# Two buffers of z made sixteen slots later, three of h, state copies behind the next exponentials, a different order of the first loads, and the second block's steps reordered

## The chip, the cores and the metric

The kernel runs on one core of one Trainium2 chip. All tensors are float32. The metric is device time in microseconds (us), the median of several runs. A separate profiled execution supplies the trace.

## The reference, cut to what matters

There are two layers on an image tensor x of shape (4, 128, 128, 128), which is batch, channel, row, column. The first layer treats each image as a sequence of L = 16384 positions:

```python
h1 = relu(xf @ mlp_w1.T + mlp_b1); xm = h1 @ mlp_w2.T + mlp_b2
x_in, z = split(xm @ in_proj_w.T, 2)                 # 256 channels each
u = silu(depthwise_conv4(x_in) + conv_b)             # causal, 4 taps
dt, Bm, Cm = split(u @ x_proj_w.T, [8, 24])
delta = softplus(dt @ dt_proj_w.T + dt_proj_b)
def step(h, inp):                                    # 256 x 16 states, over L
    dA = exp(d_t[:, :, None] * A)
    h = h * dA + d_t[:, :, None] * B_t[:, None, :] * u_t[:, :, None]
    return h, einsum('bds,bs->bd', h, C_t)
y = (scan(step) + u * D) * silu(z); out = y @ out_proj_w.T
x = silu(group_norm(out, 4 groups) * gn_w + gn_b) + x
```

The second layer filters in frequency:

```python
a = relu(agg_w @ group_norm(concat[f, f], 32 groups) + agg_b)     # f = x of layer 1
weights = softmax(mean_hw(a) @ wg_w.T + wg_b)                     # 4 per image
xf = rfft2(f); ff = rfft2(irfft2(xf * wc))                        # 4 filters wc
out = irfft2(sum_f weights_f * xf * ff) + residual_weight * f
```

## The kernel before, in words

`block0` computes the first layer. The sequence is cut into chunks of T = 512 positions, NCH = 32 for each image and 128 in all. A chunk has NP = 16 slots, and the order of the work on each engine is written out by hand: a table `todo[slot, phase]` collects small functions, and the last loop of `block0` goes through the slots in order, and in each through the phases in a fixed order. Each engine runs its own instructions in the order in which this loop emits them.

`pre(k)` prepares chunk k. `load` fetches the image part `xt`; `h1_mm`, `h1_act`, `xm_mm` and `xm_act` are the two small layers; `z_mm` and `z_act` make z and copy it out of PSUM (L212 to L221); `cv_mm` makes the convolution with four matmuls for each half of the channels; `silu_act` applies silu to u and then to z (L229 to L233). After that `xd_mm`, `dt_mm` and `dt_act` make delta, `du_pool` multiplies delta and u on POOL (L303), and the rows are written to DRAM and read back replicated (`rep_load`, L311), so that one partition holds one (channel, state) pair. The list at L313 to L324 gives each of these steps its slot, counted from the start of the chunk's own scans.

The 256 x 16 states of a chunk are treated two rows of 128 at a time, which is one `pair(n)` for each slot n. `exps(n)` is emitted one slot ahead and makes dA on ACT (L387). `dbu` makes the products delta·B·u on POOL (L354). `scans(n)` runs the recurrence on DVE (L405). In slots with p = 0 the result goes to a buffer `h`, POOL multiplies it with C (L412), and ACT copies the last column, which is the state for the next chunk (L413). In slots with p = 2 the scan works in place, DVE multiplies with C (L407) and ACT copies the last columns (L408). `by_vector` decides which. While an image's group norm runs beside the scans of the next image (`norming(k)`, 16 chunks for each of three images) one more row goes to POOL, in slot 13 of the chunk; h is then used in slots 12, 13 and 14. The pool `p2` gives `h` two buffers and `zs`, which holds z, three. `gate` multiplies y with silu(z) in slots 26 and 34, counted as in the list; `o_mm` is in slot 36.

`finish(s, io, b, ...)` is the rest of layer 1 and the weights of layer 2 for one image: `group_norm`, then for 32 parts `norm_load`, `norm_act` (silu on ACT into PSUM, L563), `norm_dve` (adds x on DVE and stores, L567) and `norm_stats` (L571), a second `group_norm`, and `agg_load`, `agg_mm`, `agg_act`. For images 0 to 2 it is spread over the slots of the next image. For image 3 it is spread over the steps of `block1`.

`block1` computes the spectral layer. A unit is 8 channels of one image, 64 units in all; a unit takes 3 steps t (3, 3 and 2 channels), and step t holds pieces of several blocks at different depths: `evict(t-8)`, `residual(t-9)`, `products(t-2)`, `conjugates(t)` on DVE; `over_h(t)`, `over_w(t-1)`, `back_h(t-7)`, `back_w(t-8)` on PE. Units of image 3 must come after its weights are known. So the first `wait` groups of channels are done for three images only and their units of image 3 are put in later, between the `rest` groups. Three of the waiting groups (`kept`) still have their filters in SBUF when image 3 follows; each of the others (`late`) has its filter, 2.08 MB, read a second time. `spare` is worked out from the last step of `finish`.

At the very start the 27 constants are read with loads that alternate between SP's and ACT's queue (`const`, L71), then a few products of them are made on DVE (L109 to L130). The first `xt` is issued by SP behind all of these; a pool of its own for the taps (`cwb`) is freed before.

Of the kernel before, what the change touches and what calls it, by code (L numbers as in the profile page):

```python
# [33 lines left out]
P = 128  # L34
T = 512
# [9 lines left out]
@with_exitstack  # L45
def kernel(ctx: ExitStack, tc: tile.TileContext, a: dict, out: bass.AP):
    nc = tc.nc
    x = a["x"]
    B, C, H, W = x.shape
    L = H * W  # L50
    NCH = L // T
    DI = a["mlp_w1T"].shape[1]
    NH = DI // P
    NS = (a["x_wT"].shape[1] - a["dt_wT"].shape[0]) // 2
    NG = NS // SQ
    ND = P // DG
    R = a["dt_wT"].shape[0]
    NX = R + 2 * NS
    KC = a["conv_wT"].shape[0]
    HALO = KC - 1  # L60
    WF = W // 2 + 1
    NF = a["wg_wT"].shape[1]

    cpool = ctx.enter_context(tc.tile_pool(name="const", bufs=1))
    dpool = ctx.enter_context(tc.tile_pool(name="dram", bufs=1, space=DRAM))
    spool = ctx.enter_context(tc.tile_pool(name="stats", bufs=2))
    opool = ctx.enter_context(tc.tile_pool(name="outs", bufs=2, space=DRAM))

    loads = [0]

    def const(name, shape, src):  # L71
        t = cpool.tile(shape, F32, tag=name, name=name)
        eng = (nc.sync, nc.scalar)[loads[0] % 2]
        loads[0] += 1
        eng.dma_start(out=t, in_=src)
        return t

    def col(name):

        n = a[name].shape[0] // P  # L80
        return const(name, [P, n], a[name].rearrange("(j p) -> p j", p=P))

    w1 = const("w1", [P, DI], a["mlp_w1T"])
    b1 = col("mlp_b1")
    w2 = const("w2", [P, NH, C], a["mlp_w2T"].rearrange("(j p) c -> p j c", p=P))
    b2 = col("mlp_b2")
    win = const("win", [P, 2 * DI], a["in_wT"])
    cb = col("conv_b")
    wx = const("wx", [P, NH, NX], a["x_wT"].rearrange("(j p) r -> p j r", p=P))
    wdt = const("wdt", [R, DI], a["dt_wT"])  # L90
    bdt = col("dt_b")
    alog = const("alog", [P, NH * NG * ND], a["alog_q"])
    sel = const("sel", [P, DG], a["c_sel"])
    dvec = col("D")
    wo = const("wo", [P, NH, C], a["out_wT"].rearrange("(j p) c -> p j c", p=P))
    gnw = col("gn_w")
    gnb = col("gn_b")
    ident = const("ident", [P, P], a["c_ident"])
    g0 = const("g0", [P, P], a["c_g0"])
    g1 = const("g1", [P, P], a["c_g1"])  # L100
    gam = col("gn_gamma")
    bet = col("gn_beta")
    wagg = const("wagg", [P, 2, C], a["agg_wT"].rearrange("(j p) o -> p j o", p=P))
    bagg = col("agg_b")
    wwg = const("wwg", [P, NF], a["wg_wT"])
    bwg = const("bwg", [P, NF], a["wg_b"].partition_broadcast(P))
    resw = const("resw", [P, 1], a["residual_weight"].partition_broadcast(P))

    eps = cpool.tile([P, 1], F32, tag="eps", name="eps")  # L109
    nc.vector.memset(eps, EPS)  # L110
    ones = cpool.tile([P, P], F32, tag="ones", name="ones")
    nc.vector.memset(ones, 1.0)

    amat = cpool.tile([P, NH * NG * ND], F32, tag="amat", name="amat")
    nc.scalar.activation(amat, alog, AF.Exp)
    nc.vector.tensor_scalar_mul(amat, amat, -1.0)
    diag = cpool.tile([P, NH, P], F32, tag="diag", name="diag")
    for j in range(NH):
        nc.vector.tensor_scalar_mul(diag[:, j, :], ident, dvec[:, j : j + 1])

    wck = cpool.tile([P, KC, DI], F32, tag="wck", name="wck")
    with tc.tile_pool(name="taps", bufs=1) as taps:
        cwb = taps.tile([P, KC, DI], F32, tag="cwb", name="cwb")
        nc.sync.dma_start(out=cwb, in_=a["conv_wT"].partition_broadcast(P))
        for t in range(KC):
            nc.vector.tensor_mul(wck[:, t, :], win[:, 0:DI], cwb[:, t, :])

    weff0 = cpool.tile([P, C], F32, tag="weff0", name="weff0")
    nc.vector.tensor_scalar_mul(weff0, wagg[:, 0, :], gam[:, 0:1])
    nc.vector.scalar_tensor_tensor(weff0, wagg[:, 1, :], gam[:, 1:2], weff0, ALU.mult, ALU.add)  # L130
    bias0 = cpool.tile([P, 1], F32, tag="bias0", name="bias0")
    wts = [cpool.tile([P, NF], F32, tag=f"wts{b}", name=f"wts{b}") for b in range(B)]

    x1 = [dpool.tile([C, H, W], F32, tag=f"x1_{b}", name=f"x1_{b}") for b in range(B)]
    x1flat = [t.rearrange("c h w -> c (h w)") for t in x1]
    xflat = x.rearrange("b c h w -> b c (h w)")

    stats, outs = {}, {}
    shared = SimpleNamespace(**{k: v for k, v in locals().items() if k not in ("ctx", "tc")})
    block0(tc, shared)  # L140
    block1(tc, shared)


def block0(tc, s):
# [4 lines left out]
    with ExitStack() as ctx:  # L149
# [18 lines left out]

        pb0 = psum("bias0")
        for j in range(2):  # L170
            nc.tensor.matmul(pb0[:, 0:1], s.wagg[:, j, :], s.bet[:, j : j + 1], start=j == 0, stop=j == 1)
        nc.vector.tensor_add(s.bias0, pb0[:, 0:1], s.bagg)

        st = {}
        stats, outs = s.stats, s.outs

        def pre(k):
# [7 lines left out]
            def load():  # L185
                xt = d["xt"] = p1.tile([P, T], F32, tag="xt", name=f"xt_{k}")
                nc.sync.dma_start(out=xt, in_=s.xflat[b, :, i * T : (i + 1) * T])

# [29 lines left out]
            def z_act():  # L218
                d["zs"] = p2.tile([P, NH, T], F32, tag="zs", name=f"zs_{k}", bufs=3)
                for j in range(NH):  # L220
                    nc.scalar.copy(d["zs"][:, j, :], ps["z", j])  # L221
# [7 lines left out]
            def silu_act():  # L229
                u = d["u"] = p2.tile([P, NH, T], F32, tag="u", name=f"u_{k}")  # L230
                for j in range(NH):
                    nc.scalar.activation(u[:, j, :], ps["cv", j], AF.Silu, bias=s.cb[:, j : j + 1])
                nc.scalar.activation(d["zs"], d["zs"], AF.Silu)  # L233

# [71 lines left out]
            def rep_load(j):  # L306
# [7 lines left out]
                (-9, "pe", load), (-7, "pe", h1_mm), (-6, "act", h1_act), (-5, "pe", xm_mm), (-4, "act", xm_act),  # L314
                (-3, "pe", z_mm), (-1, "act", z_act), (0, "pe", partial(cv_mm, 0)), (1, "pe", partial(cv_mm, 1)),
                (2, "act", silu_act), (3, "pe", xd_mm), (4, "act", xd_act), (5, "pe", dt_mm), (5, "pe", xd_turn),
                (5, "act", bc_load), (6, "act", dt_act), (7, "act", xd_turn_act), (7, "pool", partial(du_pool, 0)),
# [71 lines left out]
        def scans(n):  # L389
# [9 lines left out]
            if pool:  # L399
                h = p2.tile([P, 2, T], F32, tag="h", name=f"h_{k}_{j}_{r}_{p}")  # L400
            for q in range(2):
# [7 lines left out]
            if pool:  # L409
                q = slice(pool[0], pool[-1] + 1)  # L410
                ps = slice(p + pool[0], p + pool[-1] + 1)
                nc.gpsimd.tensor_tensor(hb[:, ps, :], h[:, q, :], d["C"][:, ps, :], ALU.mult)  # L412
                nc.scalar.copy(last[:, q], h[:, q, T - 1])  # L413

# [47 lines left out]
        for k in range(n_chunks):  # L462
            for at, phase, f in pre(k) + post(k):
                todo[at + (k - 1) * NP, phase].append(f)
        io = SimpleNamespace(big=p2, bufs=3, small=tiny, psum=psum)

# [23 lines left out]
        with tc.manual_schedule():  # L490
            for n in range(min(slots), max(slots) + 1):
                for phase in ("turn", "sums", "pe", "exps", "act", "pool", "dbu", "gate", "scans", "dve", "end"):
                    for f in todo[n, phase]:
                        f()


def group_norm(s, io, b, mat, which, stat, at, then):
# [12 lines left out]
    def mean_mm():  # L510
        ps = g["ps"] = io.psum(f"gm_{which}_{b}")
        nc.tensor.matmul(ps[:, 0:1], mat, g["mv"][:, 0:1], start=True, stop=True)

# [7 lines left out]
    def var_mm():  # L521
        ps = g["ps"] = io.psum(f"gv_{which}_{b}")
        nc.tensor.matmul(ps[:, 0:1], mat, g["q"], start=True, stop=True)

# [12 lines left out]

def finish(s, io, b, first, norm, agg):

# [88 lines left out]

    todo = group_norm(s, io, b, s.g0, 0, lambda: stats[b], first, start)
    for i in range(NCH):  # L630
        at = norm(i)
        todo += [
            (at[0], "pe", partial(norm_load, i)), (at[1], "act", partial(norm_act, i)),
            (at[2], "dve", partial(norm_dve, i)), (at[2], "end", partial(norm_stats, i)),
        ]
    c = at[2] + 5
    todo += group_norm(s, io, b, s.g1, 1, lambda: g["stat"], c, middle)
    todo += [(c + 4, "pe", bias_mm), (c + 4, "act", bias_act)]
# [13 lines left out]
def block1(tc, s):  # L652
# [10 lines left out]
    with ExitStack() as ctx:  # L663
# [29 lines left out]
        )  # L693
        t1 = 8 + NCH + 14
        todo = defaultdict(list)
        steps = finish(s, io, B - 1, 0, lambda i: (5 + i, 8 + i, 8 + i), lambda i: (t1 + i - 3, t1 + i, t1 + i, None))
        for at, phase, f in steps:
# [151 lines left out]
        with tc.manual_schedule():  # L849
            load(0)  # L850
            for t in range(3 * N + LAG + 3):
# [11 lines left out]
                evict(t - LAG - 1)  # L863
                residual(t - LAG - 2)
                products(t - 2)
                conjugates(t)
                over_w(t - 1)
# [98 lines left out]
```

## Time and profile before

| | us |
|---|---|
| median of three runs (7412.48 to 7416.26) | 7413.63 |
| the profiled execution's own time | 7411.48 |
| its span, first to last instruction | 7409.7 |
| first scan on DVE | 60.74 |
| last DVE instruction of `block0` starts | 6589.11 |
| first `conjugates` of `block1` | 6603.61 |
| DVE, POOL, ACT, PE busy over the span | 7033.2, 6896.5, 6082.8, 5982.2 |

The table divides the span into three parts: a start of 61 us, a long stretch of scans of about 6530 us, and the spectral block of about 820 us. Busy times are sums over an engine's instructions; a wait is the idle time of an engine ahead of an instruction, with the event that ended it. Most executions of a kernel agree within some tenths of a per cent.

### The profile page before, as it was taken

What the parts mean: (1) busy time and instruction counts of PE and PEld (TensorE: products, weight loads), DVE (VectorE), ACT (ScalarE), POOL (GpSimd) and SP (SyncE); (2) the same over time, 40 slices, a digit from 0 to 9 for tenths busy, and PEclk for the clock granted to TensorE, in tenths of its full rate; (3) what the DMA queues carried; (4) which work ended last, traced back from release to release, by engine and by line L of the source; (5) the groups of instructions that cost most, each with busy time, mean ns of one, the idle gap of its engine ahead of it and who ended that gap; (6) DMA issues with size and microseconds to landing.
All of it is one profiled execution on the core that took longest, in us unless ns stands there. A gap on an engine that the chain in (4) does not pass through costs nothing. (4 is left out here: it accounts for less than half of the span.)

```text
span 7409.7 us, 90629 instructions
## 1 busy us (share of the span) xinstructions
PE 5982.2 (81%) x25908; PEld 2690.3 (36%) x25908; DVE 7033.2 (95%) x8168; ACT 6082.8 (82%) x13181; POOL 6896.5 (93%) x3188
## 2 busy tenths in 40 slices
PE   7777877877878787887777788887777788867999
PEld 2332323332322233332222233332222233337999
DVE  6999999999999999999999999999999999977787
ACT  6888888888888888888888888888888888866887
POOL 6999999999999999999999999999999999976788
PEclk8888888878888889888888888988888888889999
DMA  5666666666777766667777676676776766757675
GB/s 138 159 156 146 157 156 155 147 160 164 181 178 175 181 156 166 168 163 175 176 175 182 163 174 167 159 170 173 175 183 171 175 165 157 175 148 219 176 188 154
DMA packets 855817, 1242.08 MB, mean 168 GB/s; under 512 B 78729, under 2 KB 310289, under 8 KB 855313
## 3 DMA queue, kind: packets, MB, share of 16 engines
q1 hardware_dynamic: 853200, 1236.11, 68.1%
q8 instruction: 204, 3.34, 0.2%
q14 instruction: 301, 2.46, 0.1%
q10 hardware_dynamic: 2112, 0.16, 0.0%
HBM read 992.71 MB, written 243.27 MB: 167 GB/s over the span
## 5 line engine op out<-in xcount | busy, mean ns | idle before, releaser
L354 POOL TENSOR_TENSOR hb<-rdu,rB 128x1536 f32<-128x1536 f32 (+2 forms) x1536 | 3604.4, 2363 | 32.9 <-DMA rdu<-dd 28.9
L387 ACT ACTIVATE da<-rdelta,amat 128x512 f32<-128x512 f32 x4096 | 2669.9, 694 | 3.8 <-issue 0.7
L412 POOL TENSOR_TENSOR hb<-h,rC 128x1024 f32<-128x1024 f32 (+1 forms) x1072 | 2436.1, 2275 | 235.3 <-DVE h L405 217.4
L405 DVE TENSOR_TENSOR_SCAN da<-da,st,hb 128x512 f32<-128x512 f32 x1976 | 2421.6, 1269 | 7.3 <-POOL hb L354 5.3
L426 PE MATMUL y<-hb,sel 128*32 128x512 f32 x8192 | 1332.5, 726 | 2.9 <-POOL hb L412 2.7
L405 DVE TENSOR_TENSOR_SCAN h<-da,st,b 128x512 f32<-128x512 f32 x992 | 1262.2, 1272 | 73.8 <-POOL du L303 33.6
L407 DVE TENSOR_TENSOR hb<-da,rC 128x512 f32<-128x512 f32 x2040 | 1298.0, 676 | 3.0
L405 DVE TENSOR_TENSOR_SCAN h<-da,st,hb 128x512 f32<-128x512 f32 x1000 | 1254.6, 1258 | 5.7 <-ACT da L387 5.7
L374 PE MATMUL b<-ident,bt 128*128 128x128 f32 x4096 | 770.5, 313 | 575.5 <-DVE h L405 484.3
L227 PE MATMUL pp_cv<-xm,wck 128*128 128x512 f32 x2048 | 1051.1, 660 | 35.6 <-ACT zs L221 34.7
L374 PEld LDWEIGHTS b<-ident,bt 128*128 128x128 f32 x4096 | 563.4, 160 | 1147.7 <-DVE h L405 746.5
L295 ACT ACTIVATE bt<-pt_dut,xdt 128x256 f32<-128x256 f32 x2048 | 834.5, 469 | 146.2 <-PE pt_dut L284 146.2
L408 ACT COPY st<-da 128x1 f32<-128x1 f32 x2040 | 280.5, 161 | 644.6 <-DVE hb L407 638.7
L227 PEld LDWEIGHTS pp_cv<-xm,wck 128*128 128x128 f32 x2048 | 412.9, 213 | 739.0 <-issue 464.1
L192 PE MATMUL pp_h<-xt,w 128*128 128x512 f32 x512 | 398.0, 922 | 285.3 <-DMA xt<-in_x 259.5
L751 POOL TENSOR_TENSOR wb<-wb,term 128x1040 f32<-128x1040 f32 x192 | 461.3, 2403 | 153.9 <-ACT term L745 143.9
L284 PE MATMUL pt_dut<-ident,du 128*128 128x128 f32 x1024 | 211.8, 331 | 277.0 <-ACT st L408 267.0
L422 PE MATMUL y<-u,diag 128*128 128x512 f32 x512 | 301.1, 673 | 108.1 <-DVE zs L436 107.8
L413 ACT COPY st<-h 128x2 f32<-128x2 f32 (+1 forms) x1072 | 207.0, 193 | 180.9 <-DVE h L405 176.0
L303 POOL TENSOR_TENSOR du<-delta,u 128x512 f32<-128x512 f32 x256 | 319.3, 1269 | 37.4 <-ACT delta L266 37.4
L387 ACT ACT_TABLE_LOAD x261 | 334.9, 1283 | 2.9
L284 PEld LDWEIGHTS pt_dut<-ident,du 128*128 128x128 f32 x1024 | 129.8, 160 | 567.9 <-POOL du L303 428.2
(137 smaller groups left out, 8038.0 us busy)
## 6 DMA issues: line engine op xcount, KB each, us to landing
rdelta<-dd SPq DMA_DIRECT2D x1024, 256.0 KB, 4.8
rdu<-dd SPq DMA_DIRECT2D x1024, 256.0 KB, 7.8
rC<-bc SPq DMA_DIRECT2D x512, 256.0 KB, 7.6
rB<-bc SPq DMA_DIRECT2D x512, 192.0 KB, 4.7
dd<-delta SPq DMA_DIRECT2D x256, 256.0 KB, 7.6
dd<-du SPq DMA_DIRECT2D x256, 256.0 KB, 6.7
ft<-in_filt_w SPq DMA_DIRECT2D x96, 520.0 KB, 7.0
xt<-in_x SPq DMA_DIRECT2D x128, 256.0 KB, 7.5
```

Of the source, the lines that this page charges most:

```text
L192: nc.tensor.matmul(ps["h", j], s.w1[:, j * P : (j + 1) * P], d["xt"], start=True, stop=True)
L227: nc.tensor.matmul(ps["cv", j], w, d["xm"][:, t : t + T], start=t == 0, stop=t == KC - 1)
L284: nc.tensor.transpose(ps["dut"][:, 2 * t + j, :], d["du"][:, j, at : at + P], s.ident)
L295: nc.scalar.activation(d["bt"][:, 2 * h + t, :, q, :], src, AF.Copy, scale=d["xdt"][:, 2 * h + t, R + q : R + q + 1])
L354: nc.gpsimd.tensor_tensor(hb[:, p : p + n, :], d["du", j][:, m : m + n, :], d["B"][:, p - 1 : p - 1 + n, :], ALU.mult)
L374: nc.tensor.transpose(b[:, t * P : (t + 1) * P], src, s.ident)
L387: nc.scalar.activation(d["da", p][q], d["delta", j][:, m, :], AF.Exp, scale=s.amat[:, c : c + 1])
L405: nc.vector.tensor_tensor_scan(o, das[q], b, init, ALU.mult, ALU.add)
L407: nc.vector.tensor_tensor(hb[:, p + q, :], das[q], d["C"][:, p + q, :], ALU.mult)
L412: nc.gpsimd.tensor_tensor(hb[:, ps, :], h[:, q, :], d["C"][:, ps, :], ALU.mult)
L426: nc.tensor.matmul(y[m * DG : (m + 1) * DG, :], s.sel, d["hb", j, r][:, p, :], start=False, stop=r == NG - 1)
L751: nc.gpsimd.tensor_tensor(wb, wb, u[n].terms[f], ALU.add)
```

## The change

The z matmuls, the copy of z out of PSUM and silu of z are moved to slots 13, 15 and 18 of the chunk, 16 slots later; in the list silu of z becomes a step of its own (`z_silu`). `zs` gets two buffers, `h` three. The copies at L413 go into a new phase `late` of the next slot, which stands behind `exps`. The constants are all issued by SP, in three parts: w1 ahead of everything, those that the first chunk needs in the first slot (`first_constants`), the others in slot 4 and the products of those in slot 8 (`later_constants`, `later_products`). The first image part is issued by ACT. `conv_wT` is read directly into `wck` and multiplied in place. The small tiles of `finish` in `block0` have one buffer instead of two. In `block1`, `conjugates(t)` stands ahead of `products(t-2)`; the 32 norm parts take two of every three steps, and the addition and the store of a part come one step after its silu, behind `products`; the stages behind them start later.

```diff
     def const(name, shape, src):
         t = cpool.tile(shape, F32, tag=name, name=name)
-        eng = (nc.sync, nc.scalar)[loads[0] % 2]
-        loads[0] += 1
-        eng.dma_start(out=t, in_=src)
+        nc.sync.dma_start(out=t, in_=src)
         return t
...
+    def first_constants(s):
+        s.b1 = col("mlp_b1")
+        s.w2 = const("w2", ...)
+        s.b2 = col("mlp_b2")
+        win = s.win = const("win", [P, 2 * DI], a["in_wT"])
+        wck = s.wck = const("wck", [P, KC, DI], a["conv_wT"].partition_broadcast(P))
...     (cb, wx, wdt, bdt, ident, alog, D, sel, in this order)
+        for t in range(KC):
+            nc.vector.tensor_mul(wck[:, t, :], win[:, 0:DI], wck[:, t, :])
+        nc.scalar.activation(amat, alog, AF.Exp)
...
+    def later_constants(s):
...     (wo, gnw, gnb, g0, g1, gam, bet, wagg, bagg, wwg, bwg, resw; memsets of eps and ones)
+    def later_products(s, psum):
+        nc.vector.tensor_scalar_mul(weff0, s.wagg[:, 0, :], s.gam[:, 0:1])
+        nc.vector.scalar_tensor_tensor(weff0, s.wagg[:, 1, :], s.gam[:, 1:2], weff0, ALU.mult, ALU.add)
...     (bias0: two matmuls and an addition)
...
-                nc.sync.dma_start(out=xt, in_=s.xflat[b, :, i * T : (i + 1) * T])
+                (nc.sync if k else nc.scalar).dma_start(out=xt, in_=s.xflat[b, :, i * T : (i + 1) * T])
...
-                d["zs"] = p2.tile([P, NH, T], F32, tag="zs", name=f"zs_{k}", bufs=3)
+                d["zs"] = p2.tile([P, NH, T], F32, tag="zs", name=f"zs_{k}")
...
                     nc.scalar.activation(u[:, j, :], ps["cv", j], AF.Silu, bias=s.cb[:, j : j + 1])
+            def z_silu():
                 nc.scalar.activation(d["zs"], d["zs"], AF.Silu)
...
-                (-3, "pe", z_mm), (-1, "act", z_act), (0, "pe", partial(cv_mm, 0)), (1, "pe", partial(cv_mm, 1)),
-                (2, "act", silu_act), (3, "pe", xd_mm), ...
+                (0, "pe", partial(cv_mm, 0)), (1, "pe", partial(cv_mm, 1)), (2, "act", silu_act),
+                (NP - 3, "pe", z_mm), (NP - 1, "act", z_act), (NP + 2, "act", z_silu), (3, "pe", xd_mm), ...
...
-                h = p2.tile([P, 2, T], F32, tag="h", name=f"h_{k}_{j}_{r}_{p}")
+                h = p2.tile([P, 2, T], F32, tag="h", name=f"h_{k}_{j}_{r}_{p}", bufs=3)
...
-                nc.scalar.copy(last[:, q], h[:, q, T - 1])
+                todo[n + 1, "late"].append(partial(nc.scalar.copy, last[:, q], h[:, q, T - 1]))
...
-        io = SimpleNamespace(big=p2, bufs=3, small=tiny, psum=psum)
+        todo[min(n for n, _ in todo), "end"].append(partial(s.first_constants, s))
+        todo[4, "end"].append(partial(s.later_constants, s))
+        todo[8, "end"].append(partial(s.later_products, s, psum))
+        io = SimpleNamespace(big=p2, bufs=3, small=p1, psum=psum)
...
-                for phase in ("turn", "sums", "pe", "exps", "act", "pool", ...
+                for phase in ("turn", "sums", "pe", "exps", "late", "act", "pool", ...
...
-            (at[2], "dve", partial(norm_dve, i)), (at[2], "end", partial(norm_stats, i)),
+            (at[2], add, partial(norm_dve, i)), (at[2], "end", partial(norm_stats, i)),
...
-        t1 = 8 + NCH + 14
+        def norm(i):
+            t = 9 + 3 * (i // 2) + i % 2
+            return t - 3, t, t + 1
+        t1 = norm(NCH - 1)[2] + 14
-        steps = finish(s, io, B - 1, 0, lambda i: (5 + i, 8 + i, 8 + i), lambda i: (t1 + i - 3, t1 + i, t1 + i, None))
+        steps = finish(s, io, B - 1, 0, norm, lambda i: (t1 + i - 3, t1 + i, t1 + i, None), "add")
...
                 residual(t - LAG - 2)
+                conjugates(t)
                 products(t - 2)
-                conjugates(t)
+                for f in todo[t, "add"]:
+                    f()
                 over_w(t - 1)
```

## The prediction

> **What bounds the kernel now.** I read the page first, then DVE's waits, then the windows by stage, then the timeline where a wait sits.
>
> ```profile
> PE 5982.2 (81%) x25908; PEld 2690.3 (36%) x25908; DVE 7033.2 (95%) x8168; ACT 6082.8 (82%) x13181; POOL 6896.5 (93%) x3188
> ```
>
> This is the page's first part, busy time by engine. DVE and POOL are nearly full, so a gain can only come from DVE's idle time, or from a stage that another engine sets. The windows show which stages those are (columns: length, then busy time of PE, PEld, DVE, ACT, POOL, clock, DMA):
>
> ```profile
> 160.00:1000.00 840.00, 669.09 (x2547) 253.22 (x2540) 830.23 (x865) 696.60 (x1513) 811.06 (x370) 0.84 0.66 154
> 6637.00:6813.00 176.00, 129.31 (x987) 121.70 (x986) 131.57 (x281) 114.04 (x220) 101.17 (x52) 0.94 0.75 230
> 6870.00:7009.00 139.00, 139.00 (x1071) 124.18 (x1071) 95.62 (x221) 113.68 (x252) 102.39 (x54) 1.00 0.63 178
> 7009.00:7285.00 276.00, 275.78 (x2454) 275.30 (x2453) 227.69 (x539) 227.36 (x466) 245.75 (x127) 1.00 0.67 178
> ```
>
> The scans (first line, as an example of 62 to 6580) leave DVE 1.2% idle; POOL is at 96.6%, so behind DVE's gap stands POOL's. In block 1, from 6813 on, PE is full (third and fourth line). The one loose stage is 6637 to 6813, the 32 norm parts of image 3: no engine is above 75%. DVE's waits say where its idle time lies (us in total, times, longest):
>
> ```profile
> DVE h L405 <- ACT da L387: 57.1, 18, 46.4
> DVE of L567 <- ACT pf_n L563: 43.5, 21, 4.1
> DVE h L405 <- POOL du L303: 35.1, 122, 0.5
> DVE h L405 <- POOL hb L412: 24.5, 37, 1.5
> ```
>
> 46.4 of the first is the start. The second is the loose stage. The last two are the scans' own.
>
> **The change part by part.** The sum is made against the profiled execution, 7411.5 us (span 7409.7 and 1.8 around it). The median is 2.1 above it.
>
> *Start.* The chain to the first scan at 60.74 begins with these rows:
>
> ```profile
> 9.64 0.23 ACT L115 ACTIVATE amat<-alog 128x32 f32<-128x32 f32 x1
> 14.32 0.33 SPq L187 DMA_DIRECT2D xt<-in_x  x1
> 17.02 3.75 PE L192 MATMUL pp_h<-xt,w 128*128 128x512 f32 x4 [6.01 <-DMA xt<-in_x]
> 24.33 1.99 PE L216 MATMUL pp_z<-xm,win 128*128 128x512 f32 x4 [0.78 <-ACT xm L210]
> 26.16 7.12 PE L227 MATMUL pp_cv<-xm,wck 128*128 128x512 f32 x16
> ```
>
> xt is issued at 14.32, when the products of the taps are done, and arrives 2.7 us later. Afterwards ACT issues it at about 0.7, so h1_mm can start near 4. But on ACT `amat` now stands between xt and h1_act and waits for alog, the twelfth load on SP. SP's constants left at 0.74 to 8.85, 14 of them, 0.62 each, beside as many on ACT; alone, four loads of L311 leave in 1.75, 0.44 each. So alog leaves at 0.74 + 11 x (0.44 to 0.62) = 5.6 to 7.6 and lands 2.5 later (ident: 5.58 to 8.06), at 8.1 to 10.1. h1_act follows at 8.4 to 10.4 instead of 19.11: 8.7 to 10.7 earlier. Its second half no longer waits for PE (1.0), and cv follows xm_act without z between (26.16 - 24.33 = 1.8). Against that, the matmuls after the gap may run at the slow rate that L192 shows (3.75 for four) instead of that of z (1.99): up to 1.8. From cv on the chain is the same. I take -12 (-8 to -14).
>
> A rule bears on this. "DMA: Bandwidth & Descriptors", section Issuing engines are not separate DMA queues, says that issuing from several engines saves only issue time. By that, one queue costs twelve issues ahead of alog, which is in the sum; if the shared engines set the pace instead, 0.30 for each load over both queues, alog would land at 6.9 and the start would give -14. The row 0.44 is for a lone queue and is the one I use.
>
> *Later constants and products.* Twelve loads on SP in slot 4 (12 x 0.44 = 5.3 us) hold up bc_load, dt's stores and du's of chunk 1, needed by dbu in slot 14, some 28 us later; SP already waits far longer there for ACT. Cost 0; if that cover were gone, 5 us once. On DVE eps, ones, weff0 and bias0 (0.06 + 0.17 + 0.29 + 0.34 + 0.16 = 1.0) move from the idle start into the full stage: +1.0. Here a rule speaks against the change: "SBUF — State Buffer", section SBUF: two separate sides, says that DVE and GpSimd hold a shared port pair for a whole instruction when DVE has two SBUF inputs, and the other blocks. The rows of before show weff0 at 0.29 and 0.34, but with POOL idle; the scans and L407 read one operand from PSUM, so no row shows the conflict. By the rows this is +1; by the rule two instructions wait for a POOL operation of up to 3.4 us each, +8. I take +3. The two tiny matmuls have PE's slack of 20%.
>
> *Three buffers of h.*
>
> ```profile
> 1863.84 3.58 POOL L412 TENSOR_TENSOR hb<-h,rC 128x1024 f32<-128x1024 f32 x2
> 1866.23 1.28 DVE L405 TENSOR_TENSOR_SCAN h<-da,st,b 128x512 f32<-128x512 f32 x1 [0.62 <-POOL hb L412]
> ```
>
> In a norming chunk h is used in slots 12, 13 and 14. With two buffers the scan of slot 14 waits until POOL has read that of slot 12: 1863.84 + 2.36 = 1866.20. With three it reuses slot 10's, long read. da and b were ready at 1864, so all of the wait goes: 34 such rows x 0.62 = -21, and three in the first chunks (1.46, 0.53, 1.46), of which I take -2. Next to be late is POOL: 50.0 us of work in a chunk of 52; enough room.
>
> *State copies behind the exps.* The rows "POOL du" are not for du. h has no operand from it; the same moment is the end of the exponential:
>
> ```profile
> 3225.36 1.27 ACT L266 ACTIVATE delta<-pp_dt,dt_b 128x512 f32<-128x512 f32 x2
> 3226.51 0.19 ACT L413 COPY st<-h 128x2 f32<-128x2 f32 x1
> 3226.72 1.28 ACT L387 ACT_TABLE_LOAD   x1
> 3228.02 1.30 ACT L387 ACTIVATE da<-rdelta,amat 128x512 f32<-128x512 f32 x2
> 3228.83 1.28 DVE L405 TENSOR_TENSOR_SCAN h<-da,st,b 128x512 f32<-128x512 f32 x1 [0.28 <-POOL du L303]
> ```
>
> Slot 6's copy stands in ACT's chain softplus, copy, table load, exp, and the scan waits 0.28 at its end. Without it the table load starts at the end of softplus, 3226.63, not 3226.72: 0.09 earlier (0.19, if all of the copy counts). 122 x 0.09 = -11 (-11 to -23). Elsewhere the copies don't matter: ACT waits 176 us at L413 for the scan, and the exp behind it needs the same scan to free its PSUM bank, so the wait changes hands only.
>
> *z later.* The same instructions in the same slots, for the chunk before. z_silu (1.04) now stands ahead of u's two silus; the table load, the sum and the exps behind are the same, and u's wait for cv (18.6 in all) is filled. The scans of slot 4 with a small wait ("POOL hb L354", 15.1 in 18) may gain: -2. u and xd_mm are up to 1.0 later, two slots ahead of softplus; PE's slack hides it. gate needs z in slot 26, eight slots on. SP's and POOL's order doesn't change. Scans together: -36 (-18 to -48).
>
> *Block 1.* The norm steps t = 8 to 55 of before take 242 us (conjugates at 6633.55 and 6875.82): 5.5 a step for 32, 4.0 for the rest. PE needs 3.59 a step. DVE's work is 8.8 for three steps (227.69 / 276 x 10.77) and 1.33 for an addition with its stats. Before, three parts fall on three steps, 12.8, and DVE waits 3.4 for silu of the same step (2.49 + 0.94): 16.4 observed. After, two parts: 8.8 + 2.7 = 11.5, and silu is a step ahead. A new wait comes in, though. ACT's `wb` needs the products of the step before it may be overwritten:
>
> ```profile
> 6696.25 1.16 ACT L745 ACTIVATE wb<-ft,wts 128x1040 f32<-128x1040 f32 x1 [1.31 <-DVE pr L804]
> ```
>
> Behind conjugates the products end 0.5 later. In that step two terms (2.1), silu (0.7) and the next copy of pa (0.36) queue behind wb on ACT, 3.2 with handover 3.4; DVE has addition, stats, evict and residual meanwhile, 2.3, and then waits 1.1 for conjugates. So 12.6 for three steps, 4.2 a step: 48 x 4.2 = 201. The later group norm's stalls (16 x 0.45 = 7) come afterwards instead. Gain 242 - 201 - 7 = 34. Outside the norm the same loop is 8.8 - 1.0 + 2.7 + 0.2 = 10.7 against PE's 10.77: just covered, I take +3 (0 to +13). `spare` grows from 33 to 38 units, so 13 groups wait instead of 11 and ten filters instead of eight are read twice: 4.2 MB at the end, where four units in a row each need 2.08 + 1.05 MB in 10.8 us, 290 GB/s; slices of that rate are there now (300). Prefetched four units ahead; +4 (0 to +15). Block 1: -34 + 3 + 4 = -27 (-50 to +3).
>
> **Sum:** -12 + 3 - 36 - 27 = -72. 7411.5 - 72 = 7339.5, and 2.1 for the median: 7342 (rounded up).
>
> **The rivals.** (a) Block 1 stays as it was: transfers grow to some 3.2 MB for a unit in the norm steps, 255 GB/s at 12.6 us against 230 now, and the x1 tile, fetched one unit ahead, arrives late. For it: slices at 300 in that stage. Against: a landing of 5.3 us. Then -12 + 3 - 36 = -45: 7369. (b) The scans don't gain: POOL, at 96.6%, becomes their limit as soon as DVE stops waiting, or the copies do nothing since the exps wait for the same scan. -12 + 3 - 27 = -36: 7378. (c) Block 1 does better: the wb wait is absorbed by the buffers; 11.5 for three steps, 48 x 3.83 = 184, and ACT's 0.19 counts in full: 7342 - 17 - 11 = 7314. (d) Slower: the loop products, wb, two terms, copy of pa, conjugates is longer than PE's 10.77 in every unit. It decides from about 12.1 a unit: 1.36 x 64 = 87 eats the 72 and 15 more. At 12.4, 48 units outside the norm cost 78 and the norm gains 34 - 26: -45 + 78 - 8 + 4 = +29: 7443. Against it: ACT waits at wb only ten times now, 15.4 us, none in the PE-bound steps.
>
> **How the numbers follow.** Main case 52%, c 18%, a 12%, b 11%, d 4%, others in between 3%. The median of this kernel can be told from no change at about 0.2%, 15 us. Main, a, b and c are all beyond it: 0.93 faster; 0.03 the same; 0.04 slower. The main case's own range from the bounds is 7312 to 7378; with c's own bounds it reaches down to 7298, with a's and b's up to 7380.
>
> **What would show it.** h1_act at about 9 and the first scan near 49; no "POOL hb L412" waits in norming chunks; du waits at 0.2 instead of 0.28; "of <- ACT pf_n" nearly gone, "sa <- ACT sa" larger; norm steps at 4.2. It is wrong if PE in the last 250 us falls below 97%, if h waits for POOL by another name, or if the first scan stays above 55.

## The result, and the profile after

The changed kernel takes 7341.45 us (median of six runs, 7335.76 to 7353.53), the kernel before 7412.58 in the same session (7405.85 to 7416.26). The ratio is 0.9905, with a 95% interval of 0.9895 to 0.9916. The forecast was 7342. The profiled execution took 7341.55 us, 69.93 less than that of before. The total came out as forecast, but several terms did not, and their errors cancelled: that the sum fits so closely is luck.

The page's first part, busy time by engine:

```profile
PE 5890.0 (80%) x25908; PEld 2648.4 (36%) x25908; DVE 7022.4 (96%) x8168; ACT 6064.9 (83%) x13183; POOL 6896.1 (94%) x3188
```

DVE and POOL do the same work in 70 us less. The windows by stage, moved by the 60 us that block 1 now starts earlier, show where (length, then busy time of PE, PEld, DVE, ACT, POOL, clock, DMA):

```profile
160.00:1000.00 840.00, 670.14 (x2577) 254.06 (x2573) 836.69 (x874) 700.30 (x1531) 818.57 (x374) 0.85 0.66 155
6577.00:6753.00 176.00, 152.44 (x1293) 147.80 (x1292) 151.99 (x337) 138.98 (x273) 131.94 (x68) 0.99 0.81 243
6810.00:6949.00 139.00, 137.62 (x1090) 125.48 (x1089) 94.97 (x227) 114.34 (x250) 104.37 (x55) 1.00 0.64 179
6949.00:7225.00 276.00, 268.68 (x2322) 263.96 (x2321) 211.03 (x509) 218.53 (x452) 232.02 (x120) 0.99 0.65 173
```

In the scans DVE is idle for 3.3 of 840 us; it was 9.8. The norm steps are denser (PE 152 of 176 instead of 129). In the last line, however, PE has lost 7 us where it was full before. That is a new stall. DVE's waits (us in total, times, longest) begin now with:

```profile
DVE sa L787 <- ACT sa L782: 152.5, 112, 5.5
DVE h L405 <- ACT da L387: 52.8, 26, 41.3
```

The rows "POOL du", "POOL hb L412" and "of <- ACT pf_n" are gone; the forecast had them gone or smaller. Of the second line 41.3 is the start.

Cut at five events on DVE, the two profiles give:

| stretch | before, us | after, us | difference |
|---|---|---|---|
| to the first scan | 60.74 | 51.89 | -8.85 |
| first scan to first gate (`zs`, L436) | 35.48 | 43.80 | +8.3 |
| first gate to last gate | 6489.01 | 6427.58 | -61.4 |
| last gate to first conjugates | 18.38 | 20.19 | +1.8 |
| block 1: first conjugates to the last DVE instruction | 802.0 | 791.95 | -10.05 |

The start's gain is lost again within 45 us. DVE's timeline shows the place:

```profile
79.25 1.20 DVE L405 TENSOR_TENSOR_SCAN h<-da,hb 128x512 f32<-128x512 f32 x1
80.36 9.08 DVE L126 TENSOR_SCALAR weff<-wagg,gn_gamma 128x128 f32<-128x128 f32 x1
89.48 0.35 DVE L127 SCALAR_TENSOR_TENSOR weff<-wagg,gn_gamma,weff 128x128 f32<-128x128 f32 x1
```

The first product takes 9.08 us; before, at the idle start, it took 0.29. It is not listed as a wait, because the stall counts as busy time. POOL's timeline beside it:

```profile
80.11 3.42 POOL L354 TENSOR_TENSOR hb<-rdu,rB 128x1536 f32<-128x1536 f32 x1
83.50 2.34 POOL L412 TENSOR_TENSOR hb<-h,rC 128x1024 f32<-128x1024 f32 x1
85.81 3.55 POOL L354 TENSOR_TENSOR hb<-rdu,rB 128x512 f32<-128x512 f32 x2
95.85 2.35 POOL L412 TENSOR_TENSOR hb<-h,rC 128x1024 f32<-128x1024 f32 x1 [6.49 <-DVE h L405]
```

DVE's product ends at 89.44. POOL's back-to-back operations end at 89.36, where it runs dry, since it needs the next scan from DVE. The product waited for the four consecutive POOL operations of the first three rows, not for one. Its operand was not late: `wagg` was issued at 72.6 and landed 2.4 us later.

Block 1 by its steps (start of `conjugates`): steps 8 to 56 fell from 242.3 to 208.1 us (4.34 a step); steps 56 to 102, with the second group norm, rose by 3.4; steps 102 to 191 rose from 320.4 to 337.6; what is left at both ends rose by 3.5, of which 2.1 lie in the first eight steps and 1.4 behind the last `conjugates`. In a norm step the wait at `wb` appears, as forecast with 1.1 us. The timeline, all engines:

```profile
6701.18 0.76 DVE L812 TENSOR_TENSOR pr<-sq,wb 128x260 f32<-128x260 f32 x2
...
6701.98 1.16 ACT L753 ACTIVATE wb<-ft,wts 128x1040 f32<-128x1040 f32 x1 [0.27 <-DVE pr L812]
...
6703.04 1.15 ACT L753 ACTIVATE term<-ft,wts 128x1040 f32<-128x1040 f32 x1
...
6705.19 0.42 DVE L787 TENSOR_TENSOR sa<-pa,c_sign 128x256 f32<-128x256 f32 x1 [1.08 <-ACT sa L782]
```

`wb` has to wait for the products, the second term and the copy `sa` queue behind it on ACT, and DVE waits 1.08 for `sa`.

In the late steps the stall is on PE. SP's issues ahead of one of these stalls, PE at its end, and SP's waits for a filter's buffer (window 7040 to 7300):

```profile
7094.47 0.38 SPq L855 DMA_DIRECT2D out<-ot  x1
7101.02 3.48 SPq L740 DMA_DIRECT2D ft<-in_filt_w  x4
7104.59 1.89 SPq L746 DMA_DIRECT2D xt<-x  x1
```

```profile
7111.62 1.64 PE L780 MATMUL pa<-c_fh,xt 128*128 128x130 f32 x6 [3.32 <-DMA xt<-x]
```

```profile
SPq L740 <- ACT term L753: 18.2, 3, 6.1
```

SP is to issue a filter that is needed units later. It waits 6.1 us for the filter's buffer, which ACT still reads, then issues the four parts, and only then the image tile that the next unit needs. There are three such waits and three late tiles: these units take 14.53, 13.83 and 15.77 us instead of 10.77. PE waits 11.6 us in the three together, and it resumes slowly: two `px` matmuls take 0.64 us behind the gap at 7111 and 0.39 ahead of it, and the units that follow take 11.97 to 12.36. Four parts issued without such a wait (5.34 us at 7084.26) left PE no wait above 0.4 us.

### The profile page after: what moved, and what is told of

The parts are those of the page before. It is cut to its first block, busy times and chain, and to the rows that moved or that the text cites. A ratio compares the mean times of both kernels' runs of the same rounds, so it can differ in the third digit from the quotient of the medians.

```text
span 7339.5 us, 90375 instructions
## 1 busy us (share of the span) xinstructions
PE 5890.0 (80%) x25908; PEld 2648.4 (36%) x25908; DVE 7022.4 (96%) x8168; ACT 6064.9 (83%) x13183; POOL 6896.1 (94%) x3188
## 4 chain that ended last, share of the span: by engine, by line
DVE 16%; ACT 14%; DMA 14%; PE 12%; issue 5%; POOL 2%; SPq 1%; DVEq 0%; ACTq 0%; POOLq 0%
DVE da L405 7%; ACT da L387 6%; DVE h L405 4%; DMA rdelta<-dd 3%; DMA xt<-in_x 3%; DVE hb L407 2%; PE pp_h L190 2%; DMA of<-ob 2%; ACT bt L295 1%; DMA dd<-delta 1%; DMA rB<-bc 1%; PE pa L780 1%; DMA xr<-in_x 1%; ACT L387 1%; PE y L426 1%
## 5 line engine op out<-in xcount | busy, mean ns | idle before, releaser
L412 POOL TENSOR_TENSOR hb<-h,rC 128x1024 f32<-128x1024 f32 (+1 forms) x1072 | 2433.5, 2272 | 179.2 <-DVE h L405 162.5
L426 PE MATMUL y<-hb,sel 128*32 128x512 f32 x8192 | 1313.3, 717 | 3.1 <-POOL hb L412 2.7
L225 PE MATMUL pp_cv<-xm,wck 128*128 128x512 f32 x2048 | 1018.7, 642 | 32.9 <-ACT zs L219 32.0
L374 PEld LDWEIGHTS b<-ident,bt 128*128 128x128 f32 x4096 | 548.7, 157 | 1187.2 <-DVE h L405 788.2
L190 PEld LDWEIGHTS pp_h<-xt,w 128*128 128x128 f32 x512 | 124.6, 269 | 547.2 <-DMA xt<-in_x 261.1
```

The source lines that it names most:

```text
L190: nc.tensor.matmul(ps["h", j], s.w1[:, j * P : (j + 1) * P], d["xt"], start=True, stop=True)
L225: nc.tensor.matmul(ps["cv", j], w, d["xm"][:, t : t + T], start=t == 0, stop=t == KC - 1)
L374: nc.tensor.transpose(b[:, t * P : (t + 1) * P], src, s.ident)
L426: nc.tensor.matmul(y[m * DG : (m + 1) * DG, :], s.sel, d["hb", j, r][:, p, :], start=False, stop=r == NG - 1)
```

## The experiments

Theory: the sum as predicted, with three corrections that the trace suggests (the products stand until POOL runs dry; slots 4 and 8 gain as well as slot 14; filters ahead of the tile stall PE). In the prediction's sum the third buffer and the copies together bring -34. Stage lengths below are those of the table above.

**One part of the scans undone at a time.** e1 puts the state copies back to their place and leaves three buffers of h:

```diff
-                todo[n + 1, "late"].append(partial(nc.scalar.copy, last[:, q], h[:, q, T - 1]))
+                nc.scalar.copy(last[:, q], h[:, q, T - 1])
```

> The kernel after with the state copies back in the slot of their scan; three buffers of h stay. Theory A (the copy is a link in ACT's chain softplus, copy, table load, exp that ends a wait of the scan): the scan of slot 8 starts 0.13 us later again in every chunk (1.55 us behind the multiplication before it instead of 1.42), 128 x 0.13 = 17 us slower than after, about 7358; the scan of slot 14 in norming chunks stays at 0.61. Rival B (the third buffer of h alone makes all of the gain, the copies are idle anyway): no change from after, 7341. If slot 4's 0.11 us comes from the copies too, 14 us more, 7372.

Measured: 7362.61 us, ratio 0.9933 (0.9913 to 0.9953); first to last gate 6447.9, 20 more than after. DVE's waits show the 0.3 us per chunk again, now under the name of the exponential, which supports the reading that "POOL du" had been the exponential:

```profile
DVE h L405 <- ACT da L387: 81.0, 145, 38.1
```

e2 drops `bufs=3` of h and leaves the copies late.

> The kernel after with two buffers of h; the copies stay behind the next exps. Theory A (slot 14 of a norming chunk waits for POOL to read slot 12's h): that scan starts 1.32 us behind the multiplication before it instead of 0.61, 48 x 0.71 = 34 us slower than after, about 7375; plain chunks stay at 49.9 us. Rival (a copy that comes a slot later holds h longer, so two buffers also stall plain chunks): plain chunks longer than 50.2 us, over 7390.

Measured: 7388.07, ratio 0.9971 (0.9957 to 0.9984); first to last gate 6476.0, 48 more than after. So the third buffer is the largest part, and larger than forecast.

e11 undoes both and keeps only z's place and the start of the change:

```diff
-                h = p2.tile([P, 2, T], F32, tag="h", name=f"h_{k}_{j}_{r}_{p}", bufs=3)
+                h = p2.tile([P, 2, T], F32, tag="h", name=f"h_{k}_{j}_{r}_{p}")
...
-                todo[n + 1, "late"].append(partial(nc.scalar.copy, last[:, q], h[:, q, T - 1]))
+                nc.scalar.copy(last[:, q], h[:, q, T - 1])
```

> The kernel after with two buffers of h and the copies back in their own slot; z stays later, with silu of z ahead of u. Theory A (buffer and copies make all of the scans' gain of 61.4 us from first to last gate): 6489 us between the gates as before, about 7403. Rival B (z's later place has a share of its own, 7 us or more): 6475 to 6482.

Measured: 7394.12, ratio 0.9979 (0.9968 to 0.999); first to last gate 6479.2. From here, by one profile each, the buffer alone (e1) gives 31 us, the copies alone (e2) 3, both 52: they do not simply add, since with two buffers a late copy makes slot 14 wait longer than before (table below). The two waits of before are back in DVE's list:

```profile
DVE h L405 <- POOL du L303: 35.3, 123, 0.5
DVE h L405 <- POOL hb L412: 25.4, 39, 1.5
```

The medians of the time from the start of the multiplications just ahead of the scan to the scan's start, in the three slots in question (two multiplications in slots 4 and 8, one in slot 14):

| | slot 4, plain chunks | slot 8 | slot 14, norming chunks |
|---|---|---|---|
| before | 1.30 | 1.55 | 1.32 |
| e11: both undone | 1.30 | 1.55 | 1.32 |
| e2: copies late only | 1.22 | 1.47 | 1.39 |
| e1: three buffers only | 1.24 | 1.49 | 0.61 |
| after | 1.19 | 1.42 | 0.61 |

Buffer and copies each give about half of slots 4 and 8, and the buffer alone gives slot 14. e11 equals before in all three medians: z's place changes none of them. It does change single chunks. Before, the scan of slot 4 waits more than 0.15 us in 17 plain chunks behind the first two; in e11 in 4. Summed over chunks 1 to 127, from the scan before to this scan, slot 4 takes 9.8 us less in e11 than before, as much as their first-to-last-gate times differ (6489.0 and 6479.2). So e11 speaks for its rival B, a share of z's own.

e3 leaves z's matmuls where the change puts them and moves only its silu behind that slot's other work on ACT:

```diff
-                (NP - 3, "pe", z_mm), (NP - 1, "act", z_act), (NP + 2, "act", z_silu), (3, "pe", xd_mm), ...
+                (NP - 3, "pe", z_mm), (NP - 1, "act", z_act), (NP + 2, "pool", z_silu), (3, "pe", xd_mm), ...
```

> The kernel after with silu of z behind u's two silus in the same slot, as it stood before; z itself stays 16 slots later. Theory A (silu of z ahead fills ACT's wait for the convolution, and so the exp of slot 4 comes earlier): the scan of slot 4 starts 1.29 us behind the multiplication before it instead of 1.19, 80 plain chunks x 0.11 = 9 us slower, about 7350. Rival B (slot 4's 0.11 comes from the state copies): no change, 7341.

Measured: 7347.91, ratio 0.9913 (0.9893 to 0.9933); slot 4's median stays at 1.19, so that gain does not come from z's silu. The single chunks do: nine wait 0.17 to 1.19 us in slot 4 again, and the slot's sum is 7.0 us above that of after, while in e4 to e10 it stays within 0.2 of after. So the place of z's silu makes most of z's share. The whole first-to-last-gate time, also 7 us longer, could not show it: kernels whose scans are those of after (after, e4 to e10) lie between 6421 and 6441 in their profiles.

**The start.** e4 reads the later constants in the first slot and makes their products 15 slots after it, while DVE still waits for the first scan:

```diff
-        todo[4, "end"].append(partial(s.later_constants, s))
-        todo[8, "end"].append(partial(s.later_products, s, psum))
+        todo[min(n for n, _ in todo), "end"].append(partial(s.later_constants, s))
+        todo[min(n for n, _ in todo) + 15, "end"].append(partial(s.later_products, s, psum))
```

> The kernel after with the later constants read directly behind the first ones and their products made some 15 slots before the first scan, while POOL is idle. Theory A (the 9.08 us of the first product of weff0 in slot 8 are a wait for the SBUF port that POOL holds, one operation of POOL behind the other): the product takes 0.3 us and the end comes 8 to 9 us earlier than after, about 7333. Rival B (the product waits for its operands' loads, and the scans would have waited for chunk 1 anyway): the first gate moves by less than 2 us, 7340. Rival C (the twelve loads ahead of chunk 0's own stores delay the start): the first scan is later than 51.9.

The same instruction in its profile:

```profile
14.04 0.29 DVE L126 TENSOR_SCALAR weff<-wagg,gn_gamma 128x128 f32<-128x128 f32 x1 [4.06 <-DMA wagg<-in_agg_wT]
```

The first gate comes at 82.65 instead of 95.69; 3.5 of these 13 us were there at the first scan (48.43). The median of the runs, 7338.03 (7329.34 to 7342.6; ratio 0.9899, 0.9883 to 0.9916), is only 3.4 below that of after. In the stage the gain is plain; in the time of this kernel alone it is below the scatter.

e5 makes the first product on ACT and leaves the second on DVE, in the same slot as in the change:

```diff
-        nc.vector.tensor_scalar_mul(weff0, s.wagg[:, 0, :], s.gam[:, 0:1])
+        nc.scalar.activation(weff0, s.wagg[:, 0, :], AF.Copy, scale=s.gam[:, 0:1])
```

> The kernel after with the first product of weff0 in slot 8 made by ACT (a copy with a scale) instead of DVE; the second product, which reads two operands in SBUF, stays on DVE in slot 8. Theory A (any DVE instruction with two SBUF operands waits for the port while POOL runs): the second product now shows some 9 us instead of 0.35, and the first gate is where after has it, near 95. Theory B (only the first one's form, one SBUF operand and a scalar, takes the port): the second product stays at 0.35 and the first gate comes 8 to 9 us earlier.

```profile
78.72 7.59 DVE L127 SCALAR_TENSOR_TENSOR weff<-wagg,gn_gamma,weff 128x128 f32<-128x128 f32 x1 [1.47 <-ACT weff L126]
```

One run, 7337.98. Now the second product stands, 7.59 us instead of 0.35, and ends at 86.31, again when POOL has run dry, at 86.15:

```profile
82.60 3.55 POOL L354 TENSOR_TENSOR hb<-rdu,rB 128x512 f32<-128x512 f32 x2
```

It is not the one instruction or its first use, it is POOL's unbroken row of operations.

**Block 1.** e6 puts the products ahead of conjugates again and leaves the rest of the change:

```diff
-                conjugates(t)
                 products(t - 2)
+                conjugates(t)
```

> The kernel after with conjugates behind products in block 1, as before. Theory A (conjugates ahead make the products later, and through wb and the terms the next conjugates wait 1.1 us in every three norm steps): the norm steps take 3.9 instead of 4.34 a step, 48 x 0.4 = 19 us less, and the wait of sa for ACT falls from 152 to under 50 us: about 7322. Rival B (conjugates ahead free the bank of pa earlier and that outweighs): norm steps over 4.4, 7350 or more.

Measured: 7320.0, ratio 0.988 (0.9865 to 0.9894), 21 below after. Steps 8 to 56 take 189.0 instead of 208.1, block 1 774.9 instead of 791.95. DVE's waits:

```profile
DVE sz L839 <- PE pz L834: 91.8, 109, 2.4
DVE h L405 <- ACT da L387: 52.9, 21, 39.8
DVE sa L787 <- ACT sa L782: 39.9, 25, 16.0
```

The late stalls stay (340.8 for steps 102 to 191). The 152.5 us of waits for `sa` have become 39.9, and DVE waits for PE instead, which is the engine that should set the pace here. What is behind the last `conjugates` is back at 16.9 us (18.3 in after). The reordering of conjugates thus costs time in this change and brings none.

e7 gives the norm a part in every step again, and leaves the addition one step later:

```diff
-            t = 9 + 3 * (i // 2) + i % 2
+            t = 9 + i
```

> The kernel after with a norm part in every step from 9 to 40, silu still a step ahead of the addition; 11 groups wait and eight filters are read twice, as before. DVE has 8.8 + 4.0 = 12.8 for three steps there, with the 1.1 us wait 13.9: 32 x 4.6 = 148, then 16 steps at 4.0 = 64, 212 for the 48 steps against 208 of after. Theory A (what the spread gains in the norm steps it gives back at the end, where ten filters are read twice in bursts of three and four: 17 us): the late stalls fall to about 3 us, block 1 is 10 to 15 us shorter than after, 7328. Rival B (the stalls at the end are not due to the number of filters): they stay and the result is 7345.

Measured: 7349.16, ratio 0.9914 (0.9898 to 0.9931). Steps 8 to 56 take 238.2, and the 32 of them with a part 5.3 each, where before had 5.7 and I expected 4.6. What I had left out is a late tile, in after (first line) and far more in e7 (second line; window 6570 to 6790 of both):

```profile
PE pa L780 <- DMA xt<-x: 5.7, 3, 2.6
PE pa L780 <- DMA xt<-x: 34.4, 8, 8.7
```

In e7 SP waits 73.7 us in `norm_load` (L561) for the stores of earlier parts (in after not at all), and tiles stand behind it on the same queue. So e7 does not show what the later addition is worth without the spread; the spread also keeps SP free. As in before, steps 102 to 191 take little, 318.7: `finish` ends earlier, fewer filters are read twice, and SP waits 0.9 us for a filter's buffer there instead of 18.2. So the spread gains 30 us in the norm steps and gives 19 back in the late ones.

e8 issues the tile ahead of the filters:

```diff
+                    load(n + 1)
                     for ft in loads[n]:
                         load_filter(ft)
-                    load(n + 1)
```

> The kernel after with the next unit's x1 tile loaded ahead of the filters instead of behind them on SP; nothing else. Theory A (PE waits 3 to 5 us for the x1 tile behind each burst of filters since SP issues the filter's 2.08 MB first, 5.3 us, and the tile lands behind them): the units above 10.95 us in the last 60 steps vanish, 14 to 17 us less, about 7326. Rival B (the memory's rate is the limit in the bursts, 3.1 MB in 10.8 us): the stalls move from the tile to the filters' terms, less than 5 us gained.

Measured: 7318.79 (7317.96 to 7319.18), ratio 0.9873 (0.9858 to 0.9888), 23 below after. SP's issues around the same filter, and below the window 7080 to 7260 of after and then of e8:

```profile
7090.99 1.19 SPq L746 DMA_DIRECT2D xt<-x  x1
7097.05 3.63 SPq L740 DMA_DIRECT2D ft<-in_filt_w  x4
```

```profile
7080.00:7260.00 180.00, 172.78 (x1511) 171.98 (x1510) 137.33 (x329) 139.10 (x284) 152.44 (x79) 0.98 0.78 206
```

```profile
7080.00:7260.00 180.00, 180.00 (x1614) 180.00 (x1614) 146.97 (x352) 148.76 (x305) 163.84 (x85) 1.00 0.83 221
```

SP still waits for the filter's buffer, but the tile has left before. The expectation put the delay down to the 5.3 us of issues; the trace has 3.5 us of issues and 6.1 of waiting for the buffer. The same filters and tiles are moved, at 221 instead of 206 GB/s in this window, and PE is full. It was the order on the queue, not the rate, that stalled PE. Steps 102 to 191 take 318.5, and the norm steps 203.3 instead of 208.1.

**Together.** e9 joins e4, e6 and e8, with their diffs.

> Three changes to the kernel after at once: later constants and their products made ahead of the first scan, conjugates behind products, the x1 tile ahead of the filters. If each acts in a stage of its own, the gains add: 9 at the products, 19 in the norm steps, 17 to 20 at the end, from 7341 to about 7294. Rival (with conjugates behind, the end is bound by something else than the tile, as the longer units of 13.2 to 13.7 us in that experiment suggest): under 30 us together, over 7310.

Measured: 7283.66 (7279.46 to 7284.09), ratio 0.9829 (0.9815 to 0.9844). It is the best version that differs from the change in order alone: first gate 84.16, block 1 748.5. The separate gains in time, 3.4 + 21.5 + 22.7 = 47.6, add up to less than the 57.8 measured. By stages its profile is 58.0 shorter: 11.5 up to the first gate, 43.5 in block 1, 3.0 between. e4's part is what its own time had not shown.

e10 is e9 with alog issued by ACT behind the image instead of as twelfth load on SP:

```diff
-        alog = const("alog", [P, NH * NG * ND], a["alog_q"])
+        alog = cpool.tile([P, NH * NG * ND], F32, tag="alog", name="alog")
+        nc.scalar.dma_start(out=alog, in_=a["alog_q"])
```

> The same, with alog loaded by ACT directly behind the first image part instead of twelfth on SP. Theory A (amat's wait for alog at 9.47 holds h1_act back by 1.2 us, since h1_mm ends at 8.26): h1_act starts at about 8.3 or earlier and the first scan comes 1 to 3 us earlier, 7292. Rival (the taps, landed at 8.63 and multiplied by 10.1, or the slow matmuls behind a gap, hold the chain instead): no change.

```profile
4.68 0.23 ACT L100 ACTIVATE amat<-alog 128x32 f32<-128x32 f32 x1 [1.75 <-DMA alog<-in_alog_q]
6.70 0.69 ACT L196 ACTIVATE h<-pp_h,mlp_b 128x512 f32<-128x512 f32 x1 [1.79 <-PE pp_h L191]
```

The wait for alog is gone, h1_act starts 2.2 us earlier than in e9 (8.91) and the first scan stands at 45.75 (e9: 50.01). The median, 7282.29 (ratio 0.9828, 0.9812 to 0.9845), is 1.4 below e9's, which these runs cannot tell from nothing.

## Why the prediction was right in sum and wrong in parts

| step of the sum | forecast | measured |
|---|---|---|
| start, to the first scan | -12 | -8.85 |
| later products (first scan to first gate) | +3 | +8.3 |
| scans (first to last gate) | -36 | -61.4 |
| norm steps, 242 to 201 | -41 | -34.2 |
| group norm's stalls (steps 56 to 102) | +7 | +3.4 |
| loop outside the norm, late filters (steps 102 to 191) | +3 and +4 | +17.2 |
| ends of block 1, way into it | 0 | +5.4 |
| sum | -72 | -70.2 |

*Start: right, with scatter.* alog arrived as reckoned (amat at 9.47; 8.1 to 10.1 was forecast) and h1_act began at 9.60. The first scan stands at 51.89 here, but at 47.2 to 52.2 in the nine kernels with this same start, 48.65 in their middle, so 49 was the right centre. Most of the spread is on PE: the matmuls `xm` and `cv` take 9.1 to 12.1 us together. In the profile of after they are among the slowest:

```profile
10.33 2.57 PE L200 MATMUL pp_xm<-h,w 128*128 128x512 f32 x4 [2.06 <-ACT h L195]
13.67 9.48 PE L225 MATMUL pp_cv<-xm,wck 128*128 128x512 f32 x16 [0.78 <-ACT xm L208]
```

*Later products: the rule was right, and I took the wrong end.* The row of before (0.29) came from a time when POOL was idle, so it could say nothing on the conflict. The rule of "SBUF — State Buffer" gave +8; 8.8 was lost on one instruction. Choosing +3, nearer the row, was the mistake: a row measured without the rival operation is no evidence against a rule about that rival. The rule's working was not exact either: I counted two instructions with one POOL operation each, and it was one instruction behind four.

*Scans: mechanism right, sizes too small.* Of the 61, the buffer and the copies account for 52 (e11 against after: 51.6 in the stage, 52.7 in time), and z's place for the rest. Summed over chunks 1 to 127, slot 14 of the norming chunks takes 26.6 us less, slot 8 16.0 and slot 4 19.0, together 61.6. The forecast had 21, 11 and 2, and 2 for the first chunks. In slot 8 the copies bring 0.07 to 0.08 a chunk, as reckoned (0.09); the third buffer brings 0.05 more, which the sum did not have. Slot 4 is the largest error: buffer and copies give 9 there, where they were put at nothing, and z's place gives 9.8 and was given 2. A list of waits leaves out the short ones; start-to-start gaps don't. Rival (b), no gain in the scans, is out: POOL had the room.

*Norm steps: the loop right, the tile left out.* 4.34 a step against 4.2, with the wait of 1.08 where 1.1 was forecast. Three steps without another stall take 12.67, where 12.6 was forecast. The rest is mostly the tile, for which PE waits 5.7 us here: with the tile issued first (e8) these steps take 203.3, close to the 201. So a small part of rival (a) came true in the norm steps too. Rival (c), 3.83 a step because the wait at `wb` would be absorbed, is out for the change as it is; e6, without the reordering, reaches 3.94. Rival (d) had the right chain but not its price: conjugates ahead of products costs 19 in the norm steps and 1.4 at the end, and nothing in the steps between, where PE covers it.

*Late steps: the step that failed.* The loop outside the norm costs nothing (e8: 318.5 against 320.4 before). The ten filters read twice were reckoned by rate, 290 GB/s, and priced at +4. They cost about 19 (337.6 - 318.5), because a filter that has to wait for its buffer stands on SP ahead of the tile that is needed first. That is rival (a), a late tile, mostly in another stage: the prediction looked at the rate in the norm steps and not at the order on SP in the late ones. It had said that PE below 97% in this stretch would prove it wrong; in the last 250 us it is busy for 232.8, 93%, where before had 244.7 and e8 has 244.6.

## What to carry to other kernels

Time the move of a small instruction by what runs beside it at the new place: 0.3 us in an idle start can become 9 in a full stage. On a queue, issue what is needed next ahead of what is prefetched, since a prefetch that waits for its buffer holds up all that stands behind it; the sum of the rates does not show the difference. And when a change of several parts comes out faster, undo each part: one of these cost 21 us, and two others came with a stall that a change of order takes away. Compare sums over all chunks as well as medians: a gain in a few chunks does not move a median.

## What the runs showed of the hardware that was not expected

POOL did not give way to DVE between back-to-back operations: DVE's instruction stood for 9.08 us beside four POOL operations, and for 7.59 in e5, each time until POOL had nothing left to start. The Trainium skill's page "SBUF — State Buffer" says that the one that starts first holds the pair for a whole instruction and the other blocks; here the other stayed blocked across several. The profile books that as busy time of DVE.

Slots 4 and 8 gain about 0.05 us from the third buffer alone, with no wait that the profile names. With two buffers the trace lists three semaphores that this scan waits on (PE, ACT, POOL), with three buffers two (PE, ACT). That the additional semaphore costs this time is argued from that list and not isolated by a run.

The speed of the first matmuls differs between executions of the same start: `cv` at 7.14 or 9.40 to 9.48, `xm` at 1.98 to 3.78. "TensorE: Matmul & The Clock Gate", Part 1, says that the number of slow matmuls at a start differs from run to run, since the activity window runs freely. The spread of 5 us in the first scan would fit that; no run here isolates it.
